# Layer 1's attention: column factors on GpSimd, tables two steps later, ready sums between the values' halves, last results in the values' banks

## The chip, the cores and the metric

The kernel runs on one core of one Trainium2 chip. The metric is the device time of one execution in microseconds (us), the lower the better; the time of a kernel is the median of its timed runs. One further execution is recorded by the hardware profiler, and every view of the profile and of the trace is of that execution. The engines are TensorE (PE for its matmuls, PEld for its weight loads), VectorE (DVE), ScalarE (ACT), GpSimd (POOL) and the queue SP, which only issues DMAs. The engines run beside each other; each works through its own instructions in order and waits on semaphores for what other engines make.

## The reference

Two layers on 4096 nodes with 512 features, all in float32. Layer 0 is an attention over edges with full scores; layer 1, which the change touches, has 8 heads of 64 columns. Cut to what matters:

```python
h = relu(layernorm(x)); x = x + L0(h, adj)
h = relu(layernorm(x)); x = x + L1(h, adj)

def L1(data, connectivity, W, b, src_proj, trg_proj):
    data1 = (data @ W.T + b).reshape(N, H, D)          # N, H, D = 4096, 8, 64
    src = einsum('nhd,xhd->nh', data1, src_proj)
    trg = einsum('nhd,xhd->nh', data1, trg_proj)
    e = src.T[:, :, None] + trg.T[:, None, :]
    e = where(e >= 0, e, 0.01 * e) + connectivity[None]
    scores = softmax(e, axis=-1)
    return einsum('hnm,hmd->hnd', scores, data1.transpose(1, 0, 2))
```

The connectivity that layer 1 is given is adj itself, added to the scores.

## The kernel before, in words

Layer 0 comes first (lines 89 to 687): layernorm and the two products, the scores of all pairs, and a second pass that weighs them; at its end (`tail`, `values`, `logits`) layer 1's values are left in the tile `sup` (4096 rows of 8 heads of 64 columns, also called `va`), and the two logits of each node in `s_n` and `t_m`.

Layer 1's attention (from line 692) never forms the exponent of a sum. For row n and column m of one head, exp of the leaky sum is a product of a factor of the row, a factor of the column, and max(z[n], g[m]), where z is made from the row's logit and `g_m`, `d_m` from the column's. So one score is `max(z, g) * d * exp(adj)`.

The work is cut into **8 groups**: 4 blocks of 1024 rows (`WL`) by 2 sets of 4 heads (`HG`). Each group goes through 32 **steps**, one for each 128 columns m, so there are 256 steps. In one step:

- SP loads the 128x1024 tile `e` of adj (`load`, L789), three steps ahead.
- ACT makes `ex = exp(e)` into PSUM (`exps`, L807; one buffer of two banks), `e3`, the same with head 3's factor of the column in it (`last_exps`, L817), and `rl`, relu(d z - d g) for head 0 (`relus`, L835). In four steps of a group (`BY_LOG`) head 0's weights come from one exp of a sum that a DMA has formed instead (L824, L825, L832).
- VectorE makes the four weight tiles `pr3, pr0, pr1, pr2` of 128x1024 (`weigh`, L838 to L852), each by one scalar_tensor_tensor: max(z, g) times ex or e3 (L849), and for head 0 (rl - ngd) times ex (L846). Heads 0 and 3 come out with their factor d of the column in them; heads 1 and 2 do not.
- For heads 1 and 2 the factor d goes into the values instead, in place: `scale` (L803) multiplies the 128x64 block of `va` by d. That is done once for each set of heads, so in groups 0 and 1 only, two steps ahead.
- GpSimd adds up pr3 over the columns (`acc3`, L856 and L858), and for 19 of the 32 steps (`BY_DMA`) it issues a DMA that adds pr0 to one of two sums in SBUF (`acc00` and `acc01`, L863 and L865). The last step's pr3 is left out of the sum.
- TensorE (`gather`, L867) multiplies the four weight tiles with the values: 32 instructions into four PSUM banks `pv00` to `pv11` (L881), first the pair of heads (3, 0), then the pair (1, 2). A matmul uses 32 columns of the array, so four run beside each other, and a matmul in float32 is two instructions. Then come the **denominators** into the bank `dn` (L886): heads 1 and 2 each step with the weights d, head 0 in the 13 steps that are not `BY_DMA`. In a group's last step come also pr3 of that step, and the sums acc01, acc00 and acc3. `side` changes which half of the array a step begins with, so that what one step leaves of one half can run beside the next step's start in the other.

After a group ACT copies the four banks (`os`, L910) and dn (`od`, L916). TensorE turns `od` (L920) and, one block of 128 rows a step, `os` (L936); ACT divides (L960), and a DMA of GpSimd adds to the layer's input. After the last group `finish_last` does the same at once: eight results of 128x256, `pts[0..7]`; the even ones VectorE multiplies and adds (L998), the odd ones ACT multiplies (L995), and VectorE adds the layer's input to them (L1003, L1004); four DMAs of SP write the output. `pts[0..3]` lie in the four banks of the values, `pts[4..7]` in one tile of two banks that held `ex`.

What sets the order around the change: the block runs under a manual schedule, so the order of the code is written out by hand. The start is lines 1013 to 1051: the rows' factors z of heads 3, 1, 2, 0 (`row_factors`, VectorE at L1028 and ACT at L1029), the columns' factors (L1032 to L1041), rl of step 0 (`relus(0, 0)`, L1042), memsets and copies on GpSimd (L1044 to L1047), the products of step 0 in the order of heads 3, 1, 2, 0, and the factors of steps 0 and 1. Then the loop (L1053 to L1064) issues for each step s: `load` of step s+3, `logs` of s+5, `exps` and `weigh` of s+1, `factors` and `scale` of s+2, `gather` of s, and one piece of `ending`: in group 0 that is `tables` (L750: the tables of z and u for all later groups, made from `s_n` on ACT and TensorE and written to DRAM by GpSimd's DMAs), afterwards `finish` of the group before.

Of the kernel before, what the change touches and what calls it, by code (L numbers as in the profile page):

```python
# [8 lines left out]
FP = mybir.dt.float32  # L9
# [6 lines left out]
P = 128  # L16
# [12 lines left out]
def kernel(  # L29
# [334 lines left out]
    with tc.tile_pool(name="c_a", bufs=11) as adjp, tc.tile_pool(name="c_b", bufs=4) as ebp, tc.tile_pool(  # L364
# [231 lines left out]
        def values(t):  # L596
            v = sup[:, t, :]
            nc.vector.tensor_tensor(v, vps.pop(t), wt["b"], ALU.add)
            for key, name in (("t", "ex"), ("s", "mk")):
                prs[t, key] = wkp.tile([P, BL], FP, name=name)  # L600
                eng = nc.vector if t == NT - 1 and key == "t" else nc.gpsimd
                eng.tensor_tensor(prs[t, key], v, wt[key], ALU.mult)
# [118 lines left out]

    HV = WL // BL
    JT = BL // P
    Q = P // 4
# [3 lines left out]
    with tc.tile_pool(name="p", bufs=2) as prp, tc.tile_pool(name="rl", bufs=2) as rlp, tc.tile_pool(  # L731
# [66 lines left out]
        def scale(i, m):  # L798


            if i < H // HG:
                for h in range(groups[i][1] * HG + 1, groups[i][1] * HG + 3):
                    nc.scalar.activation(va[:, m, h, :], va[:, m, h, :], AF.Copy, scale=d_m[:, h, m:m + 1])  # L803

        def exps(i, m):
            x_ = p_x.tile([P, WL], FP, name="ex")
# [31 lines left out]
        def weigh(i, m, order=ORDER):  # L838
            h = groups[i][1] * HG
            x_ = ex.pop((i, m))  # L840
            for k in order:
                if (i, m, k) in pr:
                    continue
                w = prp.tile([P, WL], FP, name=f"pr{k}", bufs=3 if k == 0 else 2)
                if k == 0:
                    nc.vector.scalar_tensor_tensor(w, rl.pop((i, m)), ngd_m[:, h // HG, m:m + 1], x_,  # L846
                                                   op0=ALU.subtract, op1=ALU.mult)
                else:
                    nc.vector.scalar_tensor_tensor(w, zs_[i, k], g_m[:, h + k, m:m + 1],  # L849
                                                   e3.pop((i, m)) if k == 3 else x_,  # L850
                                                   op0=ALU.max, op1=ALU.mult)
                pr[i, m, k] = w  # L852
            w = pr[i, m, 3]
            if m == 1:
                acc[i, 3] = acp.tile([P, WL], FP, name="acc3", bufs=1)
                nc.gpsimd.tensor_tensor(acc[i, 3], pr[i, 0, 3], w, ALU.add)  # L856
            elif 1 < m < NT - 1:
                nc.gpsimd.tensor_tensor(acc[i, 3], acc[i, 3], w, ALU.add)  # L858
            if m in BY_DMA:
                n = BY_DMA.index(m)  # L860
                if n < 2:
                    acc[i, 0, n] = acp.tile([P, WL], FP, name=f"acc0{n}", bufs=1)
                    nc.gpsimd.dma_start(acc[i, 0, n], pr[i, m, 0])  # L863
                else:
                    nc.gpsimd.dma_start(acc[i, 0, n % 2], pr[i, m, 0], accum_op=ALU.add)  # L865

        def gather(i, m):  # L867
            b, g = groups[i]
            last = m == NT - 1
            if m == 0:  # L870
                pv[i] = ([[p_v.tile([P, BL], FP, name=f"pv{c}{q}") for q in range(HV)] for c in range(2)],
                         p_v.tile([P, BL], FP, name="dn"))
            v, dn = pv[i]
            by_pe = [u for u in range(NT) if u not in BY_DMA]
            side = sum(u < m for u in by_pe) % 2
            for c, pair in enumerate(((3, 0), (1, 2))):
                for q in range(HV):
                    for r in (side, 1 - side):
                        k = pair[r]
                        for c0 in range(0, D, Q):  # L880
                            nc.tensor.matmul(v[c][q][r * D + c0:r * D + c0 + Q, :],  # L881
                                             va[:, m, g * HG + k, c0:c0 + Q],
                                             pr[i, m, k][:, q * BL:(q + 1) * BL], start=(m == 0), stop=last)

            def den(r, w, src, q, **fl):
                nc.tensor.matmul(dn[r * Q:r * Q + w.shape[1], :], w, src[:, q * BL:(q + 1) * BL], **fl)  # L886

            for r in (side, 1 - side):
                for q in range(HV):
                    hk = g * 2 + r  # L890
                    den(r * HV + q, d0_m[:, hk, m, :] if m else d0_0[:, hk, :], pr[i, m, r + 1], q,
                        start=(m == 0), stop=False)
            if m in by_pe:
                for q in range(HV):
                    den(side * HV + q, zo[:, 1 - side:3], pr[i, m, 0], q, start=False, stop=False)
            if last:
                for q in range(HV):
                    den(HV + q, zo[:, 1:3], pr[i, m, 3], q, start=False, stop=False)
                for q in range(HV):
                    den(q, zo[:, 1:3], acc[i, 0, 1], q, start=False, stop=False)  # L900
                for r, a in enumerate((acc[i, 0, 0], acc[i, 3])):
                    for q in range(HV):
                        den(r * HV + q, zo[:, 1:3], a, q, start=False, stop=True)
            for k in range(HG):
                pr.pop((i, m - 1, k), None)
            if last:
                os_ = [[osp.tile([P, BL], FP, name=f"os{c}{q}") for q in range(HV)] for c in range(2)]
                for c in range(2):
                    for q in range(HV):
                        nc.scalar.copy(os_[c][q], v[c][q])  # L910
                late[i] = os_, dn
# [60 lines left out]
        def finish_last(i):  # L972

            ys = [ep.tile([P, WT // 2, HG, D], FP, name="e") for _ in range(2)]
            for n in range(2):
                nc.sync.dma_start(ys[n], part(x1, i, n * WT // 2, WT // 2))
            yield
            dens = denominators(i)
            os_ = next(dens)
            pts = [p_v.tile([P, HG, D], FP, name=f"pv{c}{q}") for q in range(HV) for c in range(2)]  # L980
            xs = p_x.tile([P, 4, HG, D], FP, name="ex")
            pts += [xs[:, n, :, :] for n in range(4)]
            for t in range(4):
                turn(os_, t, pts[t])
            next(dens)
            for t in range(4, WT):
                turn(os_, t, pts[t])
            rd = next(dens)
            o = [prp.tile([P, WT // 2, HG, D], FP, name=f"pr{n + 1}") for n in range(2)]
            for t in range(WT):  # L990
                n, j = divmod(t, WT // 2)
                to, y = o[n][:, j, :, :], ys[n][:, j, :, :]
                if t % 2:
                    for r, k in enumerate(ORDER):
                        nc.scalar.activation(to[:, k, :], pts[t][:, r, :], AF.Copy, scale=share(rd, t, r))  # L995
                else:
                    for r, k in enumerate(ORDER):
                        nc.vector.scalar_tensor_tensor(to[:, k, :], pts[t][:, r, :], share(rd, t, r), y[:, k, :],  # L998
                                                       op0=ALU.mult, op1=ALU.add)
                if t % 2 == 0 and t:  # L1000
                    n, j = divmod(t - 1, WT // 2)
                    to, y = o[n][:, j, :, :], ys[n][:, j, :, :]
                    nc.vector.tensor_tensor(to, to, y, ALU.add)  # L1003
            nc.vector.tensor_tensor(o[1][:, WT // 2 - 1, :, :], o[1][:, WT // 2 - 1, :, :],  # L1004
                                    ys[1][:, WT // 2 - 1, :, :], ALU.add)
            for t in range(0, WT, 2):
                n, j = divmod(t, WT // 2)
                nc.sync.dma_start(part(out, i, t, 2), o[n][:, j:j + 2, :, :])
            yield
# [29 lines left out]
        for k in (1, 2, 0):  # L1039
            row_factors(k)  # L1040
        nc.vector.scalar_tensor_tensor(ngd_m, g_m[:, 0::HG, :], -1.0, d_m[:, 0::HG, :], op0=ALU.mult, op1=ALU.mult)  # L1041
        relus(0, 0)  # L1042
        for t, val in ((d0_0, 0.0), (d0_m, 0.0), (zo[:, 0:2], 0.0), (zo[:, 2:3], 1.0)):
            nc.gpsimd.memset(t, val)  # L1044
        for g in range(H // HG):
# [8 lines left out]
        for s in range(len(steps)):  # L1054
            for f, ahead in stages:
                if s + ahead < len(steps):
                    f(*steps[s + ahead])
            if s == 0:
                ending = tables()
            elif s % NT == 0:  # L1060
                ending = finish(s // NT - 1)
            if s == len(steps) - 2:
                ending = finish_last(len(groups) - 1)
            next(ending, None)  # L1064
# [36 lines left out]
```

## Time and profile before

| what | value |
|---|---|
| median of 3 runs | 2959.15 us (2958.06 to 2962.82) |
| the profiled execution's own time | 2957.07 us |
| its span | 2955.3 us |
| TensorE, busy share of the span | 99% (2911.4 us) |
| VectorE | 86% (2534.6 us) |
| ACT | 45% (1325.5 us) |
| GpSimd | 47% (1380.0 us) |
| layer 1's attention, first product of VectorE to the end | 1727.9 to 2955.3 us |
| first long run of value matmuls (L881) | from 1733.21 us |
| last denominator (L886) ends | 2943.39 us |
| L881, matmuls of the values | 8192 instructions, 594 ns each |
| L886, denominators with d of heads 1 and 2, or of pr0 | 1984 instructions of the commonest form, 592 ns each |
| L803, column factors on ACT | 128 instructions, 333 ns each |
| L858, additions on GpSimd | 232 instructions, 2406 ns each |

How to read it: the span is what lies between the first and the last instruction that the profiler saw; the time is about 1.8 us longer. Busy shares are means over all stages. Layer 1's attention is the last 1227 us of the span, and its busy times by stretch are a view of their own. In a row of the trace "pr<-z,g_m,e" names the tile written and the tiles read, "128x1024 f32" the shape, "x2" that two equal instructions are merged, and a bracket gives the idle time of the engine before it and what ended that. Matmuls are pipelined: a mean of 594 ns is a latency, and four column groups work at a time.

### The profile page before, as it was taken

How to read it: one execution, taken by the hardware profiler on the slowest of the kernel's cores; microseconds unless marked ns; L12 is line 12 of the kernel's file. 1: busy time of each engine (PE TensorE's matmuls, PEld its weight loads, DVE VectorE, ACT ScalarE, POOL GpSimd, SP SyncE). 2: the span in 40 equal slices, each digit the busy share in tenths (PEclk: the TensorE clock that was granted, in tenths of full speed). 3: DMA queues.
4: the chain of work that ended last, by engine and by line, in shares of the span. 5: the costliest groups of instructions: out<-in, count | busy, mean ns of one | idle time of the engine just before them, and what ended most of it. 6: DMA issues, size and time to landing. Idle time of an engine off the chain costs nothing.

```text
span 2955.3 us, 42955 instructions
## 1 busy us (share of the span) xinstructions
PE 2911.4 (99%) x15179; PEld 1137.7 (38%) x15179; DVE 2534.6 (86%) x3584; ACT 1325.5 (45%) x1822; POOL 1380.0 (47%) x1043
## 2 busy tenths in 40 slices
PE   8999999999999999999999989999999999999998
PEld 4444444444444444444444423323222322232222
DVE  5435777778888998998996789999999999999998
ACT  2211111111121221221221068888777777777776
POOL 3401111113444444444444756565757575757574
PEclk9999999999999999999999999999999999999999
DMA  5525666667876766756653259696969696979795
GB/s 181 172 78 200 223 218 225 226 218 187 205 178 162 177 161 187 186 166 180 190 167 127 61 152 242 187 258 188 256 191 249 194 250 204 243 202 243 208 232 153
DMA packets 485160, 570.89 MB, mean 193 GB/s; under 512 B 265080, under 2 KB 315288, under 8 KB 484944
## 3 DMA queue, kind: packets, MB, share of 16 engines
q1 hardware_dynamic: 431920, 406.70, 45.8%
q0 software_dynamic: 51008, 157.51, 23.2%
q10 hardware_dynamic: 2016, 3.93, 0.4%
q8 instruction: 119, 1.95, 0.3%
q14 instruction: 97, 0.79, 0.1%
HBM read 415.76 MB, written 72.55 MB: 165 GB/s over the span
## 4 chain that ended last, share of the span: by engine, by line
PE 92%; DVE 4%; ACT 2%; DMA 1%; issue 1%; SPq 0%; POOL 0%; DVEq 0%; ACTq 0%; POOLq 0%
PE po L480 29%; PE pv L881 27%; PE pe L331 15%; PE dn L886 9%; PE po L591 4%; PE ps L196 3%; PE pe L203 3%; DVE pr L849 2%; PE pt L936 1%; ACT e L817 1%; DMA acc<-pr 1%; DMA xt<-in_x_dram 0%; DVE acc_z L154 0%; DVE pt L441 0%; PE pt L920 0%
## 5 line engine op out<-in xcount | busy, mean ns | idle before, releaser
L881 PE MATMUL pv<-pr,sup 128*32 128x512 f32 x8192 | 1010.0, 594 | 9.0 <-POOL d_m L1046 5.4
L480 PE MATMUL po<-sup,at 128*128 128x512 f32 x2048 | 887.2, 594 | 3.8 <-DVE at L450 3.8
L858 POOL TENSOR_TENSOR acc<-acc,pr 128x1024 f32<-128x1024 f32 x232 | 558.2, 2406 | 318.1 <-DVE pr L849 317.8
L849 DVE SCALAR_TENSOR_TENSOR pr<-z,g_m,ex 128x1024 f32<-128x1024 f32 x512 | 631.0, 1273 | 5.2 <-ACT ex L807 4.1
L480 PEld LDWEIGHTS po<-sup,at 128*128 128x128 f32 x2048 | 387.1, 190 | 483.2 <-issue 446.3
L460 POOL TENSOR_TENSOR racc<-racc,ex 128x512 f32<-128x512 f32 x240 | 362.3, 1510 | 385.3 <-ACT ex L444 383.8
L881 PEld LDWEIGHTS pv<-pr,sup 128*32 128x32 f32 x8192 | 286.7, 110 | 593.2 <-issue 533.6
L444 ACT ACTIVATE ex<-d 128x512 f32<-128x512 f32 x256 | 160.5, 630 | 624.7 <-DVE d L442 616.5
L331 PE MATMUL pe<-he_t,he_t 128*128 128x512 f32 x896 | 386.4, 592 | 0.0
L807 ACT ACTIVATE ex<-e 128x1024 f32<-128x1024 f32 x256 | 263.0, 1027 | 227.2 <-DVE pr L849 226.6
L849 DVE SCALAR_TENSOR_TENSOR pr<-z,g_m,e 128x1024 f32<-128x1024 f32 x256 | 328.9, 1285 | 9.9 <-PE pv L881 5.9
L886 PE MATMUL dn<-pr,d_m 128*2 128x512 f32 x1984 | 335.6, 592 | 0.0
L817 ACT ACTIVATE e<-e,ld_m 128x1024 f32<-128x1024 f32 x256 | 291.0, 1137 | 6.5 <-DMA e<-in_adj_t_dram 6.3
L846 DVE SCALAR_TENSOR_TENSOR pr<-rl,ngd_m,ex 128x1024 f32<-128x1024 f32 x224 | 285.0, 1273 | 1.6 <-ACT ex L807 1.2
L835 ACT ACTIVATE rl<-z,ngd_m,d_m 128x1024 f32<-128x1024 f32 x224 | 275.0, 1228 | 0.0
L450 DVE TENSOR_TENSOR at<-ex,a 128x512 f32<-128x512 f32 x256 | 189.5, 740 | 71.1 <-ACT ex L444 48.0
L331 PEld LDWEIGHTS pe<-he_t,he_t 128*128 128x128 f32 x896 | 169.2, 190 | 210.1 <-issue 190.5
L335 POOL DMA_DIRECT2D e_d<-es x144 | 78.4, 545 | 364.8 <-ACT es L334 359.2
L334 ACT COPY es<-pe 128x512 f32<-128x512 f32 (+2 forms) x144 | 79.1, 550 | 377.2 <-PE pe L331 377.2
L442 DVE TENSOR_TENSOR d<-pt,mk 128x512 f32<-128x512 f32 x256 | 177.0, 691 | 8.8
L336 DVE CUSTOM_DVE_ANT_0 mk<-pe,mk 128x512 f32<-128x512 f32 (+2 forms) x144 | 93.0, 645 | 98.9 <-ACT es L334 98.8
L435 DVE TENSOR_SCALAR mk<-a 128x512 f32<-128x512 f32 x256 | 128.5, 502 | 2.2 <-DMA a<-in_adj_t_dram 2.2
(186 smaller groups left out, 2564.9 us busy)
## 6 DMA issues: line engine op xcount, KB each, us to landing
e<-in_adj_t_dram SPq DMA_DIRECT2D x256, 512.0 KB, 5.5
acc<-pr POOLq DMA_DIRECT2D x152, 512.0 KB, 5.7
a<-in_adj_t_dram SPq DMA_DIRECT2D x256, 256.0 KB, 3.8
ar<-in_adj_dram SPq DMA_DIRECT2D x120, 256.0 KB, 3.0
e_d<-es POOLq DMA_DIRECT2D x120, 256.0 KB, 3.1
eb<-e_d SPq DMA_DIRECT2D x456, 64.0 KB, 3.0
ac<-in_adj_t_dram SPq DMA_DIRECT2D x112, 256.0 KB, 3.5
et<-e_d SPq DMA_DIRECT2D x112, 256.0 KB, 3.8
```

Source lines behind the costliest of these rows:

```text
L331: nc.tensor.matmul(pe[:, :w], he_t[i][:, k, (t % TB) * P:(t % TB + 1) * P], he_t[j][:, k, BL - w:], start=(k == 0), stop=(k == KC - 1))
L450: nc.vector.tensor_tensor(w, e, aj.pop((b, m)), ALU.mult)
L460: nc.gpsimd.tensor_tensor(racc, racc, e, ALU.add)
L480: nc.tensor.matmul(po[j], w[:, j * P:(j + 1) * P], sup[:, m, :], start=(m == 0), stop=last)
L807: nc.scalar.activation(x_, ra.pop((i, m)), AF.Exp)
L817: nc.scalar.activation(x_, ra[i, m], AF.Exp, bias=ld_m[:, h // HG, m:m + 1])
L835: nc.scalar.activation(r, zs_[i, 0], AF.Relu, bias=ngd_m[:, h // HG, m:m + 1], scale=d_m[:, h, m:m + 1])
L846: nc.vector.scalar_tensor_tensor(w, rl.pop((i, m)), ngd_m[:, h // HG, m:m + 1], x_, op0=ALU.subtract, op1=ALU.mult)
L849: nc.vector.scalar_tensor_tensor(w, zs_[i, k], g_m[:, h + k, m:m + 1], e3.pop((i, m)) if k == 3 else x_, op0=ALU.max, op1=ALU.mult)
L858: nc.gpsimd.tensor_tensor(acc[i, 3], acc[i, 3], w, ALU.add)
L881: nc.tensor.matmul(v[c][q][r * D + c0:r * D + c0 + Q, :], va[:, m, g * HG + k, c0:c0 + Q], pr[i, m, k][:, q * BL:(q + 1) * BL], start=(m = ...
L886: nc.tensor.matmul(dn[r * Q:r * Q + w.shape[1], :], w, src[:, q * BL:(q + 1) * BL], **fl)
```

## The change

In groups 0 and 1 the column factors of the values (`scale`) are multiplied in by GpSimd's tensor_scalar instead of ACT's activation. For step 0, rl is made by one VectorE tensor_scalar, max(z, g) times d, ahead of the four products, instead of ACT's relu, and head 0's product of that step becomes a plain tensor_tensor. `tables` starts at step 2 instead of step 0. GpSimd now adds the last step's pr3 into acc3 too; in a group's last step TensorE takes the sums acc00 and acc3, and pr0 of that step, between the two pairs of heads, and after the second pair the denominators of heads 1 and 2 and the sum acc01; the separate denominators of pr3 are gone. In `finish_last` the eight results lie in four tiles of one bank each in the values' banks: results 0 and 2, 1 and 3, 4 and 6, 5 and 7 share a tile.

```diff
@@ scale @@
-                    nc.scalar.activation(va[:, m, h, :], va[:, m, h, :], AF.Copy, scale=d_m[:, h, m:m + 1])
+                    nc.gpsimd.tensor_scalar(va[:, m, h, :], va[:, m, h, :], d_m[:, h, m:m + 1], None, ALU.mult)
@@ weigh @@
-                if k == 0:
+                if k == 0 and (i, m) == (0, 0):
+                    nc.vector.tensor_tensor(w, rl.pop((i, m)), x_, ALU.mult)
+                elif k == 0:
                     nc.vector.scalar_tensor_tensor(w, rl.pop((i, m)), ngd_m[:, h // HG, m:m + 1], x_,
                                                    op0=ALU.subtract, op1=ALU.mult)
...
-            elif 1 < m < NT - 1:
+            elif m > 1:
                 nc.gpsimd.tensor_tensor(acc[i, 3], acc[i, 3], w, ALU.add)
@@ gather @@
-            for c, pair in enumerate(((3, 0), (1, 2))):
+
+            def values(c):
                 for q in range(HV):
                     for r in (side, 1 - side):
-                        k = pair[r]
+                        k = ((3, 0), (1, 2))[c][r]
...
+            values(0)
+            if last:
+                for r, a in enumerate((acc[i, 0, 0], acc[i, 3])):
+                    for q in range(HV):
+                        den(r * HV + q, zo[:, 1:3], a, q, start=False, stop=False)
+                if m in by_pe:
+                    for q in range(HV):
+                        den(side * HV + q, zo[:, 1 - side:3], pr[i, m, 0], q, start=False, stop=False)
+            values(1)
             for r in (side, 1 - side):
                 for q in range(HV):
                     hk = g * 2 + r
                     den(r * HV + q, d0_m[:, hk, m, :] if m else d0_0[:, hk, :], pr[i, m, r + 1], q,
-                        start=(m == 0), stop=False)
-            if m in by_pe:
+                        start=(m == 0), stop=(last and r == 1))
+            if m in by_pe and not last:
                 for q in range(HV):
                     den(side * HV + q, zo[:, 1 - side:3], pr[i, m, 0], q, start=False, stop=False)
             if last:
                 for q in range(HV):
-                    den(HV + q, zo[:, 1:3], pr[i, m, 3], q, start=False, stop=False)
-                for q in range(HV):
-                    den(q, zo[:, 1:3], acc[i, 0, 1], q, start=False, stop=False)
-                for r, a in enumerate((acc[i, 0, 0], acc[i, 3])):
-                    for q in range(HV):
-                        den(r * HV + q, zo[:, 1:3], a, q, start=False, stop=True)
+                    den(q, zo[:, 1:3], acc[i, 0, 1], q, start=False, stop=True)
@@ finish_last @@
-            pts = [p_v.tile([P, HG, D], FP, name=f"pv{c}{q}") for q in range(HV) for c in range(2)]
-            xs = p_x.tile([P, 4, HG, D], FP, name="ex")
-            pts += [xs[:, n, :, :] for n in range(4)]
+            pts = []
+            for n in range(2):
+                two = [p_v.tile([P, 2, HG, D], FP, name=f"pv{n}{c}") for c in range(2)]
+                pts += [two[c][:, j, :, :] for j in range(2) for c in range(2)]
@@ the start @@
         nc.vector.scalar_tensor_tensor(ngd_m, g_m[:, 0::HG, :], -1.0, d_m[:, 0::HG, :], op0=ALU.mult, op1=ALU.mult)
-        relus(0, 0)
+        rl[0, 0] = rlp.tile([P, WL], FP, name="rl")
+        nc.vector.tensor_scalar(rl[0, 0], zs_[0, 0], g_m[:, 0, 0:1], d_m[:, 0, 0:1], ALU.max, ALU.mult)
@@ the loop @@
             if s == 0:
+                ending = iter(())
+            elif s == 2:
                 ending = tables()
             elif s % NT == 0:
                 ending = finish(s // NT - 1)
```

## The prediction

> **What bounds the kernel now.** I read four views, in this order. First the table of stretches of layer 1's attention: length, then busy time of PE, PEld, DVE, ACT and POOL with instruction counts, the granted TensorE clock, the DMA share and GB/s.
>
> ```profile
> 1733.20:1771.00 37.80, 37.79 (x316) 10.21 (x320) 36.37 (x31) 32.94 (x54) 23.56 (x16) 0.94 0.63 170
> 1771.00:1811.00 40.00, 39.45 (x364) 11.60 (x356) 40.00 (x34) 32.53 (x45) 26.70 (x17) 1.00 0.86 212
> 1811.00:1850.00 39.00, 38.18 (x355) 12.96 (x356) 38.60 (x34) 33.84 (x46) 27.77 (x18) 1.00 1.03 278
> 1850.00:1884.60 34.60, 34.60 (x324) 11.96 (x320) 34.08 (x30) 29.23 (x43) 14.24 (x7) 1.00 0.61 177
> 1884.60:1922.00 37.40, 37.12 (x330) 11.19 (x326) 37.36 (x33) 33.46 (x60) 25.44 (x16) 1.00 0.69 185
> 2035.70:2186.70 151.00, 151.00 (x1376) 44.27 (x1372) 148.91 (x126) 116.64 (x138) 95.06 (x57) 1.00 0.84 224
> ```
>
> The first four rows are group 0 of eight, the fifth the start of group 1, the last all of group 2. TensorE is busy without a gap in group 2, and VectorE is only 2.1 us short of it. So TensorE sets the end from group 1 on, VectorE is a close second, ACT and GpSimd have room. In group 0 TensorE is idle 0.55 + 0.82 = 1.37 us, and 0.28 us at the start of group 1. So an edit that only frees ACT can win about 1.65 us, and anything more must shorten the first step, the tail or TensorE's own work.
>
> Second, the timeline of the first step, VectorE and ACT (start, length, instruction):
>
> ```profile
> 1727.90 1.28 DVE L849 SCALAR_TENSOR_TENSOR pr<-z,g_m,e 128x1024 f32<-128x1024 f32 x1
> 1729.10 2.47 DVE L849 SCALAR_TENSOR_TENSOR pr<-z,g_m,ex 128x1024 f32<-128x1024 f32 x2
> 1731.88 1.28 DVE L846 SCALAR_TENSOR_TENSOR pr<-rl,ngd_m,ex 128x1024 f32<-128x1024 f32 x1 [0.31 <-ACT rl L835]
> 1733.39 1.28 DVE L849 SCALAR_TENSOR_TENSOR pr<-z,g_m,e 128x1024 f32<-128x1024 f32 x1 [0.24 <-ACT e L817]
> 1735.91 1.28 DVE L846 SCALAR_TENSOR_TENSOR pr<-rl,ngd_m,ex 128x1024 f32<-128x1024 f32 x1 [1.24 <-ACT ex L807]
> ```
> ```profile
> 1729.53 1.04 ACT L1029 ACTIVATE z<-u 128x1024 f32<-128x1024 f32 x1
> 1730.60 1.24 ACT L835 ACTIVATE rl<-z,ngd_m,d_m 128x1024 f32<-128x1024 f32 x1
> ```
>
> The three products of heads 3, 1, 2 run while ACT still makes z of head 0; only head 0's product (L846) waits for rl. Products follow each other every 1.19 us, so a full step of four takes VectorE 4.77 us. VectorE then loses 0.24 and 1.24 us behind a loaded ACT.
>
> Third, the tail, VectorE's last results:
>
> ```profile
> 2945.64 1.63 DVE L998 SCALAR_TENSOR_TENSOR pr<-pv,rd,e 128x64 f32<-128x64 f32 x8
> 2947.18 0.42 DVE L1003 TENSOR_TENSOR pr<-pr,e 128x256 f32<-128x256 f32 x1
> 2947.51 0.85 DVE L998 SCALAR_TENSOR_TENSOR pr<-ex,rd,e 128x64 f32<-128x64 f32 x4
> 2949.42 0.86 DVE L998 SCALAR_TENSOR_TENSOR pr<-ex,rd,e 128x64 f32<-128x64 f32 x4 [0.72 <-ACT pr L995]
> 2951.27 0.43 DVE L1004 TENSOR_TENSOR pr<-pr,e 128x256 f32<-128x256 f32 x1 [0.66 <-ACT pr L995]
> ```
>
> Out of the shared tile "ex" VectorE and ACT take turns; out of "pv" both run at once. Fourth, the groups of GpSimd, for the prices below.
>
> **The change, part by part.** All sums go against the profiled execution: span 2955.3 us, time 2957.07 us. The three timed runs have a median of 2959.15 us, 2.08 above it; I carry the difference over to that median.
>
> *(a) rl of step 0 on VectorE.* The new instruction stands ahead of weigh(0, 0) in the code, and inside this block every engine ran in code order in the trace. It reads z of head 0, which ACT finishes at 1730.57. Queued behind it on VectorE are the three products that now run from 1727.90. So: start 1730.62; tensor_scalar of 128x1024 as at L1028, 0.751 us, next start 0.67 later at 1731.29; heads 3, 1, 2 at 1731.29, 1732.48, 1733.68; head 0's plain product at 1734.87 (a tensor_tensor of half the size takes 0.691 us at L442, so I keep 1.2), end 1736.1. Now that end is 1733.16. TensorE's second head of step 0 starts **2.95 us later**. ACT's next ex waits for the one PSUM tile and comes at 1736.15 to 1737.15, head 0 of step 1 at 1737.25 in place of 1735.91: VectorE itself is only 1.34 us later from there, because its 0.24 and 1.24 us stalls go. TensorE is thus 1.6 us further behind VectorE than now, which fills its 1.37 us of idle time in group 0. Net at the end of group 0: 2.95 - 1.37 = **+1.6**. ACT loses 1.23 us of work there, which nobody waits for any more.
>
> *(b) Column factors on GpSimd.* 128 activations of 0.333 us leave ACT, 128 tensor_scalars of 128x64 come to GpSimd, two a step in groups 0 and 1. The trace has none of that form. Low end: a copy of 128x4, 0.190 us (L1047). High end: the copy of 128x64 at L1046, 0.774 us, strided and run beside VectorE's first product. Between them a copy of 128x512 took 0.622 us (L247); on the line from the first, (0.622 - 0.190) / 508 per element, 64 elements take 0.24. I take 0.25, nearest to that row. GpSimd's step is then 2.41 (L858) + 0.87 (L865) + 0.5 = 3.8 of 4.77 us; 3.7 at the low end, 4.8 at the high, where it is full. Queued behind the factors are the next addition and the issue of the next accumulating DMA; these only free buffers. TensorE needs the factors two steps after they are issued. ACT's relief lets the copy of the denominators (od) come earlier, which removes the 0.28 at the start of group 1: **-0.3**.
>
> What GpSimd may cost is VectorE's time. The addition starts 1.43 us after head 3's product and ends at 3.8, the DMA issue at 4.65, so in 19 of 32 steps the two factors meet the next head-3 product at 4.77, which reads z and e3, both in SBUF. What such a meeting costs:
>
> ```profile
> 2924.34 2.39 POOL L858 TENSOR_TENSOR acc<-acc,pr 128x1024 f32<-128x1024 f32 x1 [2.66 <-DVE pr L849]
> 2926.22 1.59 DVE L849 SCALAR_TENSOR_TENSOR pr<-z,g_m,e 128x1024 f32<-128x1024 f32 x1
> ```
>
> 0.51 us of overlap made the product 0.31 us longer; at 1833.01 an overlap of 0.27 cost 0.08. Two groups of 19 steps at 0 to 0.31 are 0 to 11.8 us of VectorE; its slack of 2.1 us a group hides the first 4.2 (about 0.11 a step). I take 0.1 a step and **+0.5** for what shows; the ends are 0 and +7.6. The Trainium skill, "SBUF — State Buffer", section "Who interferes with whom", speaks against this edit: a VectorE instruction with two SBUF inputs and a GpSimd instruction that reads SBUF exclude each other for the whole instruction, the later one blocked. By that rule a product would wait at most one factor (0.25), or a factor a whole product; the sum would be about +5 if the product always lost, and -0.2 if it always won.
>
> *(c) tables from step 2.* Eight activations (0.307 each), their transposes, copies, one exp and three GpSimd DMA issues (0.88, 0.87, 0.87) move two steps, about 9 us, later, into the same kind of gaps. Their results are first loaded at step 20. Nothing passes a load on SP. **0** (bounds -0.3 to +0.3, one transpose pair on TensorE).
>
> *(d) Ready sums between the halves.* GpSimd adds the last step's head 3 (2.41 us, eight times) in a gap of 12 to 13 us in front of L856; TensorE drops two of 14 denominator products a group, four instructions. In group 2's last step the product was made at 1.28 us from 2175.72 and TensorE began that step at 2180.40, so the sum is ready 1.0 us before TensorE starts; if that lead went, the second half would wait for VectorE anyway. But does TensorE gain? Four instructions on four column groups take 0.43 us; these take turns by halves of the array. Before, the last step and what is left of step 30 make 16 half blocks that alternate, 8 x 0.86 = 6.9 us, as the chain shows (3.43 + 3.42). Now there are 15, but the last one (acc01) uses the same half as the next group's first values, so half the array stands idle: 8 x 0.86 again. **0**; lower end 7 x 0.43 = -3.0 if it packs. Two waits go: VectorE's 0.5 us per group on head 3's buffer, off the path.
>
> *(e) Last results in the values' banks.* VectorE and ACT now read separate tiles. From 2945.64 VectorE needs 16 products at 0.193 and four additions of about 0.36: 4.55, to 2950.2 in place of 2951.7. ACT's 16 at 0.217 end at 2949.1, ahead. The 3.6 us from the last addition to the end stay. **-1.5** (bounds -2.1, ACT and VectorE perfectly apart, to 0).
>
> Sum: +1.6 - 0.3 + 0.5 + 0 + 0 - 1.5 = **+0.3**: 2957.4 for the profiled execution, 2959.4 against the median.
>
> **Rivals.** *Order:* if the factor of (a) is placed behind the three products, head 0 ends at 1733.46 (+0.3), VectorE gains 1.3, and TensorE's idle 1.37 goes: -1.0 in place of +1.6, 2956.9. For it: pick (L778) ran ahead of an earlier line at the boundary of two blocks; against: inside the block no instruction did. *Packing:* (d) pays its 3.0: 2956.4. Against it: half blocks fit the measured 6.85 us. Both together: 2953.9. *Slower, the shared read:* the head-3 products lose 0.3 a step to the factors: (11.8 - 4.2) = +7.6 in place of +0.5, 2966.5; it decides from 0.11 us a step. For it the 1.59 row; against it, the typical overlap is nearer 0.25, where the rows show 0.05 to 0.08.
>
> **How the numbers follow.** Forecast 0.55, order 0.14, packing 0.13, both 0.06, shared read 0.12. About 0.2% (5.9 us) is what a measurement of this kernel can tell from no change. "Both" lies at that bound and I count it as faster, the shared read as slower, the rest within: 0.06, 0.82, 0.12. The range takes in the case "both" with scatter below and most of the shared read: 2953 to 2966.
>
> **What would show it.** (a) right: VectorE's first product after 1731, TensorE's first long run of pv near 1736; wrong: a product at 1727.9. (b): GpSimd tensor_scalar near 0.25 us, head-3 products of groups 0 and 1 with a mean under 1.38 us; (d): groups 2 to 6 still 151.05 us apart; 150.6 means packing. (e): no wait of VectorE on ACT after 2946, and about 10.4 us from the last dn to the end in place of 11.9. A GpSimd price near 0.8, or a TensorE wait on GpSimd in front of pv, would make the whole wrong.

## The result, and the profile after

The changed kernel takes **2964.18 us** (median of 19 runs, 2962.2 to 2968.54) beside 2958.06 us (19 runs, 2954.96 to 2962.82) for the kernel before on the same chip. The ratio is 1.0023, 95% interval 1.0016 to 1.0029: about 6 to 7 us slower, 4.7 to 8.6 by the interval. The forecast was 2959.4, so the time lies 4.8 us above it, inside the range, at the edge of "within 0.2%" and nearest to the rival of the shared read (2966.5). As a difference from the kernel before, the forecast was +0.3 and the measurement +6.1: with 19 runs the median of before is 1.1 us lower than the one that the forecast was added to. The profiled execution took 2964.42 us, span 2962.6.

The stretches of layer 1's attention in the changed kernel, columns as in the prediction (length, then busy PE, PEld, DVE, ACT, POOL). The first three rows have the limits of three rows shown of before; the last is all of group 2, which starts 8 us later here:

```profile
1771.00:1811.00 40.00, 40.00 (x373) 11.62 (x369) 40.00 (x35) 28.61 (x30) 39.95 (x34) 1.00 0.93 210
1811.00:1850.00 39.00, 37.45 (x340) 11.91 (x336) 39.00 (x32) 27.71 (x26) 39.00 (x33) 1.00 1.02 263
1850.00:1884.60 34.60, 33.78 (x312) 11.14 (x307) 34.54 (x28) 24.58 (x24) 31.97 (x29) 1.00 0.69 193
2044.10:2195.10 151.00, 151.00 (x1372) 47.46 (x1368) 148.69 (x126) 116.71 (x138) 97.32 (x58) 1.00 0.84 224
```

GpSimd, the fifth busy time, went from 26.70 and 27.77 to 39.95 and 39.00 us: it is full. VectorE, nearly full before (40.00 and 38.60), is full too, and TensorE is idle for 1.55 and 0.82 us in the second and third rows, where it was idle for 0.82 and 0. Group 2, which has no factors, is as before but for GpSimd's one addition more (97.32 in place of 95.06 us).

Three groups of instructions from 1725 to 2035 us, which is nearly all of groups 0 and 1 (busy us, mean ns, idle before), and below them two rows of the kernel before from the same stretch:

```profile
L859 POOL TENSOR_TENSOR acc<-acc,pr 128x1024 f32<-128x1024 f32 x59 | 162.2, 2750 | 8.6 <-DVE pr L850 8.5
...
L802 POOL TENSOR_SCALAR sup<-sup,d_m 128x64 f32<-128x64 f32 x128 | 125.0, 1410 | 0.2
L850 DVE SCALAR_TENSOR_TENSOR pr<-z,g_m,e 128x1024 f32<-128x1024 f32 x64 | 93.1, 1455 | 0.0
```
```profile
L858 POOL TENSOR_TENSOR acc<-acc,pr 128x1024 f32<-128x1024 f32 x58 | 139.7, 2409 | 79.6 <-DVE pr L849 79.3
...
L849 DVE SCALAR_TENSOR_TENSOR pr<-z,g_m,e 128x1024 f32<-128x1024 f32 x66 | 84.7, 1284 | 2.0 <-ACT os L910 1.1 <-PE pv L881 0.7 <-ACT e L817 0.2
```

A column factor takes 1410 ns in the mean, not 250; the addition 2750 in place of 2410; the head-3 product 1455 in place of 1284. GpSimd's idle time before its additions falls from 79.6 to 8.6 us. The positions at which TensorE turns the denominators (L920, now L926) place the loss: the way from the first row factor (L1028, L1035) to the end of group 0 is 5 us longer, group 1 takes 154.97 us in place of 151.05, groups 2 to 7 together are 0.2 us longer than before, and the tail is 1.1 us shorter.

How a loss arises, from the timeline of GpSimd and VectorE in group 0 (start, length, row), with VectorE's row at the spot of the first product in the kernel before below:

```profile
1833.12 1.31 POOL L824 DMA_DIRECT2D lg<-in_adj_t_dram  x1
...
1833.74 3.12 POOL L859 TENSOR_TENSOR acc<-acc,pr 128x1024 f32<-128x1024 f32 x1
1835.17 2.79 DVE L850 SCALAR_TENSOR_TENSOR pr<-z,g_m,e 128x1024 f32<-128x1024 f32 x1
...
1840.42 1.44 POOL L866 DMA_DIRECT2D acc<-pr  x1
1841.08 2.35 POOL L802 TENSOR_SCALAR sup<-sup,d_m 128x64 f32<-128x64 f32 x2
1841.45 1.27 DVE L850 SCALAR_TENSOR_TENSOR pr<-z,g_m,e 128x1024 f32<-128x1024 f32 x1
...
1843.00 2.77 POOL L859 TENSOR_TENSOR acc<-acc,pr 128x1024 f32<-128x1024 f32 x1
```
```profile
1833.01 1.36 DVE L849 SCALAR_TENSOR_TENSOR pr<-z,g_m,e 128x1024 f32<-128x1024 f32 x1
```

Read the last four rows of the changed kernel first, a normal step: two factors meet the head-3 product, the product keeps its 1.27 us, and the pair, 0.86 us when free, takes 2.35. The addition behind it starts later. GpSimd's rows overlap: the pair's row begins 0.37 us ahead of the product, while the issue of the accumulating DMA before it (L866) still runs to 1841.86. So the start of a GpSimd row does not tell when its work begins, and part of the means above is queueing behind the row before. The first rows are a step of `BY_LOG`: VectorE makes three products in place of four, GpSimd has a load to issue, and the late addition is still running when the next head-3 product is due. Now the product waits, 2.79 us in place of 1.36 at this spot before. The meeting costs VectorE nothing where the factor loses and 1.5 us where the addition wins. The Trainium skill, "SBUF — State Buffer", section "Who interferes with whom", states that whichever of the two comes later is blocked for the whole instruction. The first rows agree: the addition ends at 1836.86, and the product that began during it ends 1.1 us behind that. In the last rows the starts do not tell which came first.

The long products have a place. In each of groups 0 and 1 the products of steps 18, 22 and 26, right behind the `BY_LOG` steps 17, 21 and 25, take 2.64 to 2.79 us: 8.9 us of the 11.1 by which products are longer than before in these two groups. Behind step 29, after the last accumulating DMA of a group, the product takes 1.33 and 1.32. The other 2.2 us lie on six products of 1.44 to 1.93 us, one in group 0 and five in group 1. Shortly before each of them GpSimd has one more DMA to issue, for a `BY_LOG` load (L824) or a result of group 0 (L969).

The start and the tail stand in two more pieces of VectorE's timeline in the changed kernel:

```profile
1729.93 0.81 DVE L1050 TENSOR_SCALAR rl<-z,g_m,d_m 128x1024 f32<-128x1024 f32 x1 [2.61 <-ACT z L1036]
1730.66 1.28 DVE L850 SCALAR_TENSOR_TENSOR pr<-z,g_m,e 128x1024 f32<-128x1024 f32 x1
...
1734.24 1.21 DVE L845 TENSOR_TENSOR pr<-rl,ex 128x1024 f32<-128x1024 f32 x1
```
```profile
2954.16 1.63 DVE L1005 SCALAR_TENSOR_TENSOR pr<-pv,rd,e 128x64 f32<-128x64 f32 x8
2955.70 0.42 DVE L1010 TENSOR_TENSOR pr<-pr,e 128x256 f32<-128x256 f32 x1
2956.03 0.85 DVE L1005 SCALAR_TENSOR_TENSOR pr<-pv,rd,e 128x64 f32<-128x64 f32 x4
```

The products of heads 3, 1, 2 wait 2.61 us for z of head 0, as worked out; the tail has no wait on ACT left.

### The profile page after: what moved, and what is told of

Read it like the earlier page. It is cut to its first block, busy times and chain, and to the rows that moved or that the text cites. A ratio compares the mean times of both kernels' runs of the same rounds, so it can differ in the third digit from the quotient of the medians.

```text
span 2962.6 us, 42943 instructions
## 1 busy us (share of the span) xinstructions
PE 2914.6 (98%) x15147; PEld 1146.7 (39%) x15147; DVE 2545.9 (86%) x3585; ACT 1295.6 (44%) x1693; POOL 1494.5 (50%) x1179
## 4 chain that ended last, share of the span: by engine, by line
PE 82%; POOL 6%; DVE 5%; DMA 3%; issue 2%; ACT 1%; SPq 1%; DVEq 0%; POOLq 0%; ACTq 0%
PE po L480 29%; PE pv L883 20%; PE pe L331 15%; PE dn L888 7%; PE po L591 4%; PE ps L196 3%; POOL acc L859 3%; DVE pr L850 3%; PE pe L203 3%; DMA acc<-pr 2%; POOL sup L802 1%; POOL acc L866 1%; PE pt L942 1%; DVE pr L847 0%; SPq L409 0%
## 5 line engine op out<-in xcount | busy, mean ns | idle before, releaser
L883 PE MATMUL pv<-pr,sup 128*32 128x512 f32 x8192 | 1024.2, 595 | 15.2 <-DVE pr L850 12.0
L859 POOL TENSOR_TENSOR acc<-acc,pr 128x1024 f32<-128x1024 f32 x240 | 597.7, 2490 | 264.9 <-DVE pr L850 263.1
L883 PEld LDWEIGHTS pv<-pr,sup 128*32 128x32 f32 x8192 | 293.5, 110 | 598.2 <-issue 521.0
L850 DVE SCALAR_TENSOR_TENSOR pr<-z,g_m,e 128x1024 f32<-128x1024 f32 x256 | 339.6, 1327 | 4.2 <-PE pv L883 4.0
L866 POOL DMA_DIRECT2D acc<-pr x136 | 133.1, 978 | 2.2 <-DVE pr L850 1.2
```

Of the source, the lines that this page charges most:

```text
L883: nc.tensor.matmul(v[c][q][r * D + c0:r * D + c0 + Q, :], va[:, m, g * HG + k, c0:c0 + Q], pr[i, m, k][:, q * BL:(q + 1) * BL], start=(m = ...
```

## The experiments

Every kernel was timed beside the kernel before on one chip, whose medians were 2957.71 (first four), 2957.62 (next four) and 2958.53 us (last four). "Over before" is the difference of the medians, with the ratio's 95% interval. "Long products" is the time by which head-3 products of groups 0 and 1 over 1.41 us exceed 1.28 us, added up in the profiled execution; it is 0 in the kernel before.

| kernel | us | over before | ratio | long products, groups 0 + 1 |
|---|---|---|---|---|
| changed kernel | 2964.18 | +6.1 | 1.0016 to 1.0029 | 4.7 + 6.4 |
| e1 factors on ACT | 2958.65 | +0.9 | 0.9992 to 1.0010 | 0 |
| e2 start undone | 2960.89 | +3.2 | 1.0003 to 1.0021 | 4.8 + 6.2 |
| e3 factors ahead of the DMA | 2964.95 | +7.2 | 1.0013 to 1.0036 | 0.5 + 0.3 |
| e4 factors alone | 2964.41 | +6.7 | 1.0013 to 1.0031 | 4.9 + 5.3 |
| e5 tail alone | 2956.77 | -0.9 | 0.9987 to 1.0006 | 0 |
| e6 late factors on ACT | 2958.83 | +1.2 | 0.9996 to 1.0013 | 0.3 + 1.7 |
| e7 early factors on ACT | 2963.95 | +6.3 | 1.0013 to 1.0031 | 4.5 + 4.5 |
| e8 rl behind, factors on ACT | 2955.43 | -2.2 | 0.9986 to 1.0003 | 0 |
| e9 sums and tables alone | 2957.44 | -1.1 | 0.9987 to 1.0005 | 0 |
| e10 start alone | 2959.99 | +1.5 | 0.9992 to 1.0009 | 0 |
| e11 two factors in one | 2958.85 | +0.3 | 0.9993 to 1.0011 | 0.7 + 0.7 |
| e12 rl behind, and the tail | 2955.62 | -2.9 | 0.9984 to 1.0001 | 0 |

**Which part loses.** e1, e2 and e4 take one part away or put one in; e3 keeps the work and changes its order on GpSimd.

e1:
```diff
-                    nc.gpsimd.tensor_scalar(va[:, m, h, :], va[:, m, h, :], d_m[:, h, m:m + 1], None, ALU.mult)
+                    nc.scalar.activation(va[:, m, h, :], va[:, m, h, :], AF.Copy, scale=d_m[:, h, m:m + 1])
```

> The changed kernel with the 128 column factors back on ACT; all else as changed. Theory A (shared read): a factor and a head-3 product, which both read SBUF, shut each other out; GpSimd gets full in groups 0 and 1, its late additions then hold up head-3 products. Of the 5.0 us that group 0 got longer A gives 3.4 to this and of group 1 all 3.9: expected 2957 (7.3 under the changed kernel), long head-3 products gone from groups 0 and 1, GpSimd back to about 27 of 40 us. Theory B (start): the loss comes from rl of step 0 on VectorE, which VectorE never makes good: expected 2963 to 2964, group 1 still near 155. Theory C (only the sheer amount of GpSimd work counts) gives the same as A here.

Measured 2958.65: 5.2 us back by the differences from before, and no long product left. That is 1.7 us above what A gave, which e1's interval still holds. The profiled execution (2960.16, the slowest of the eleven) also shows 4.7 us of ACT waits for loads of adj in group 0, so its positions are not compared. B falls.

e2:
```diff
-        rl[0, 0] = rlp.tile([P, WL], FP, name="rl")
-        nc.vector.tensor_scalar(rl[0, 0], zs_[0, 0], g_m[:, 0, 0:1], d_m[:, 0, 0:1], ALU.max, ALU.mult)
+        relus(0, 0)
...
-                if k == 0 and (i, m) == (0, 0):
-                    nc.vector.tensor_tensor(w, rl.pop((i, m)), x_, ALU.mult)
-                elif k == 0:
+                if k == 0:
```

> The changed kernel with only the start undone: rl of step 0 on ACT again and head 0's product as before. Theory A: the start costs 1.6 to 3.0, so 2961.2 to 2962.6; group 1 stays near 155 us. If GpSimd sets the pace of group 0, the earlier start is partly lost again and the gain is under 1.6. Theory B: 5 us or more come back, 2959 or less, and group 1 is 151 again.

Measured 2960.89, 2.9 under the changed kernel by the differences from before. Group 1 stays at 154.8 us. Both speak for A.

e4 is the diff of e1 the other way round, on the kernel before.

> The kernel before with the column factors on GpSimd and nothing else changed. Theory A: 5 to 7 us over before, 2963 to 2966, factors with a mean over 1 us and long head-3 products in groups 0 and 1. Theory B: within 1 us of before.

Measured 2964.41, +6.7, factors with a mean of 1418 ns: the factors alone make the whole loss. In e4's trace groups 0 and 1 are 2.9 and 4.0 us longer than before. On the scale of the first row factor its head-3 products fall behind those of the kernel before by 1.4 to 1.5 us at steps 19, 23 and 27 of group 0 and 19 and 27 of group 1, each right behind a long product, and far less elsewhere.

e3:
```diff
             elif m > 1:
                 nc.gpsimd.tensor_tensor(acc[i, 3], acc[i, 3], w, ALU.add)
+            if (i, m) > (0, 0) and (i, m) != steps[-1]:
+                scale(*steps[steps.index((i, m)) + 1])
             if m in BY_DMA:
...
-        stages = ((load, 3), (logs, 5), (exps, 1), (weigh, 1), (factors, 2), (scale, 2), (gather, 0))
+        stages = ((load, 3), (logs, 5), (exps, 1), (weigh, 1), (factors, 2), (gather, 0))
```

> The changed kernel with the two factors of a step issued between GpSimd's addition and its accumulating DMA, so that they come some 3.8 us after the head-3 product in place of 4.7, ahead of the next head-3 product. The same instructions on the same engines. Theory A: the mean factor falls from 1.41 to about 0.45 to 0.6 us, GpSimd is free 5 us or more in 40, and 5 to 7 of the 7.3 us come back: 2957 to 2959. Theory C (amount of work): the same time as the changed kernel, 2964. Theory B: 2964.

Measured 2964.95, from only six runs that spread from 2958.93 to 2968.32: in the median none of the time came back, against A as first put. The groups of instructions show why that isn't simply theory C:

```profile
L850 DVE SCALAR_TENSOR_TENSOR pr<-z,g_m,e 128x1024 f32<-128x1024 f32 x64 | 83.0, 1297 | 0.8 <-PE pv L885 0.7
...
L802 POOL TENSOR_SCALAR sup<-sup,d_m 128x64 f32<-128x64 f32 x128 | 72.5, 693 | 0.0
```

The mean factor halves to 693 ns, and head-3 products are nearly as short as before. In the profiled execution group 1 takes 152.21 us, 2.8 less than in the changed kernel, so there most of its loss is gone; group 0 is 1.1 us longer than there. In it another wait took the place. Of ACT's waits in group 0 the longest:

```profile
ACT pr L831 <- DMA acc<-pr: 4.4, 1, 4.4
```

The accumulating DMA, now behind the factors, releases one of the three buffers of pr0. In step 25, where ACT writes pr0 itself, it waits 4.43 us for that; the exp behind it is late, and VectorE idles 3.66 us. That wait was 0.6 us in the changed kernel and 0 before. So there seem to be two ways in which a late GpSimd costs time; the second rests on this one wait. The DMA that it waits for is that of step 22: its issue took 2.38 us in place of 0.87 before, and it landed 9.0 us after that, its counterparts 7.3 (before) and 7.1 us (changed kernel). So late issue and slow transfer both have a part; the exact shares stay open.

**Where it loses.** A full step of 4.77 us leaves 3.5 us outside the head-3 product; the addition and two free factors take 2.39 + 0.86 = 3.25. A `BY_LOG` step has one product less, 3.6 us, and leaves 2.3. The four such steps are 17, 21, 25 and 29; that is theory A2. (In the traces the products behind the first three are the long ones, as said above.) e6 puts the factors from step 16 on back on ACT, e7 those up to step 15:

```diff
+                    if m < 16:
                         nc.gpsimd.tensor_scalar(va[:, m, h, :], va[:, m, h, :], d_m[:, h, m:m + 1], None, ALU.mult)
+                    else:
+                        nc.scalar.activation(va[:, m, h, :], va[:, m, h, :], AF.Copy, scale=d_m[:, h, m:m + 1])
```

> The changed kernel with the factors of steps 16 to 31 of groups 0 and 1 on ACT, those of steps 0 to 15 on GpSimd. Theory A2: a full step of four products leaves GpSimd 3.5 us of 4.8 outside VectorE's head-3 product, which holds an addition of 2.4 and two factors of 0.43; the shorter steps 17, 21, 25 and 29, with three products and a load issued by GpSimd, do not, and all of the loss falls there. Expected: 4.5 to 6 us under the changed kernel, 2958 to 2959.5 on the scale of a kernel before at 2957.7. Theory A as first put (each of the 64 steps loses alike): half comes back, about 3 us, 2961. Theory C (amount of GpSimd work): the same as A, half.

> The mirror image: factors of steps 0 to 15 on ACT, those of steps 16 to 31 on GpSimd. Theory A2: nearly all of the loss stays, 0 to 1.5 us under the changed kernel, 2962.5 to 2964. Theories A as first put and C: half comes back, 2961.

Measured 2958.83 and 2963.95. The same number of GpSimd instructions costs nothing that can be told from e1 in the first half of a group, and everything in the second. The groups from 1811 to 1890 us, the second half of group 0, in e6 and then in e7:

```profile
L862 POOL TENSOR_TENSOR acc<-acc,pr 128x1024 f32<-128x1024 f32 x16 | 38.7, 2420 | 21.4 <-DVE pr L853 21.4
L853 DVE SCALAR_TENSOR_TENSOR pr<-z,g_m,e 128x1024 f32<-128x1024 f32 x18 | 23.2, 1287 | 0.0
```
```profile
L862 POOL TENSOR_TENSOR acc<-acc,pr 128x1024 f32<-128x1024 f32 x15 | 41.5, 2768 | 2.6 <-DVE pr L853 2.6
...
L853 DVE SCALAR_TENSOR_TENSOR pr<-z,g_m,e 128x1024 f32<-128x1024 f32 x17 | 26.3, 1548 | 0.0
```

The addition's idle time of 21.4 us shrinks to 2.6, and the head-3 product gets 0.26 us longer in the mean. In the first half of e6's group 0 GpSimd is nearly as full as in the changed kernel (its addition idles for 3.7 us in 76, 2.6 there), and only one product of 1.59 us pays for it; in group 1 four pay 1.7 us together. Theory C, which gave both half of the loss, falls with that, and A as first put too. The halves differ in more than the short steps, so it is the place of the long products, steps 18, 22 and 26 in e7 too, that ties the loss to them.

**The price of a factor.** e11 makes the two factors of a step in one instruction:

```diff
-                for h in range(groups[i][1] * HG + 1, groups[i][1] * HG + 3):
-                    nc.gpsimd.tensor_scalar(va[:, m, h, :], va[:, m, h, :], d_m[:, h, m:m + 1], None, ALU.mult)
+                h = groups[i][1] * HG + 1
+                nc.gpsimd.tensor_tensor(va[:, m, h:h + 2, :], va[:, m, h:h + 2, :],
+                                        d_m[:, h:h + 2, m:m + 1].to_broadcast([P, 2, D]), ALU.mult)
```

> The changed kernel with the two factors of a step in one GpSimd instruction of 128x128 (a product of two tensors, the second spread along the columns) in place of two of 128x64. Estimate from the addition of 128x1024 at 2.39 and the small copies at 0.19: about 0.5 us for both in place of 0.86. Theory A2 (GpSimd's need in the shorter steps sets the loss): 0.36 us less in each of the 32 late steps, a fourth to a half of the 5.3 us comes back: 2961.5 to 2963. If the loss hangs on the meeting of any factor with the head-3 product, however short: 2964.

Measured 2958.85, 5.8 us better than the changed kernel by the differences from before, more than either theory gave. Its timeline around a `BY_LOG` step:

```profile
1812.43 0.72 POOL L802 TENSOR_TENSOR sup<-sup,d_m 128x128 f32<-128x128 f32 x1
1812.78 1.22 POOL L825 DMA_DIRECT2D lg<-in_adj_t_dram  x1
1812.84 1.40 DVE L851 SCALAR_TENSOR_TENSOR pr<-z,g_m,e 128x1024 f32<-128x1024 f32 x1
1814.16 2.46 DVE L851 SCALAR_TENSOR_TENSOR pr<-z,g_m,ex 128x1024 f32<-128x1024 f32 x2
1814.40 2.39 POOL L860 TENSOR_TENSOR acc<-acc,pr 128x1024 f32<-128x1024 f32 x1 [0.39 <-DVE pr L851]
```

The one instruction has started before the product, so the product waits for what is left of it and is 0.12 us longer, and GpSimd is free again when the addition may start. With two instructions the second mostly came after the product had begun and waited for all of it (the median factor of the changed kernel takes 1764 ns). The first one's row is mostly as long, though it begins 0.2 to 0.4 us ahead of the product; why it loses there is not shown. Free of a product the one takes 0.39 us against 2 x 0.43: of the 1.6 us between 2.35 and 0.72 only 0.5 are the price; the rest is the meeting with the product.

**The other parts.** e5 is the diff of `finish_last` alone, e9 those of `gather`, of the last addition and of `tables`, e10 that of the start, each on the kernel before.

> The kernel before with the last results in the values' banks and nothing else changed. Expected from the changed kernel's trace, where the way from the last group's denominators to the end is 1.2 us shorter than before: 1.2 under before (0.9 to 1.5), in the profile no wait of VectorE on ACT between its last results. Rival: VectorE's time between the last results was hidden by the stores, 0.

> The kernel before with the ready sums between the values' halves and the tables from step 2 on, nothing else changed. Both stand at 0 in the sum on record: within 0.15% of before (2953.5 to 2962), groups 2 to 6 as far apart as before. Packing rival: 3.0 less. Tables rival: the table's bytes and loads come two steps later, into the stretch in which the DMA engines are full, and cost 1 to 2 us in groups 0 and 1.

> The kernel before with only the start changed: rl of step 0 on VectorE ahead of the three products. The sum on record has +1.6. With e1_factors_act at +0.94 over before, which holds the shorter tail (-0.9 to -1.2), the start is worth +1.8 to +2.2 by that run: 2959.5 to 2960 where before is 2957.7. If the start is harmless by itself, 2957.7.

Measured -0.9, -1.1 and +1.5 us, none of them told from 0 by its interval. They lie at or near what the expectations have, e9 nearer 0 than the packing's -3.0, which its interval still holds. The traces say more: in e9 groups 2, 4 and 6 take 151.05 us as before and 3 and 5 are no shorter, against the packing; its group 0 is 0.1 us longer, and group 1 1.2, which is no sign of the tables, since e10, where they are not moved, has the same 1.2. In e10 group 0 is 1.4 us longer. With e4's +6.7 the four medians add up to +6.2, the changed kernel has +6.1; that this fits so closely is luck, since each of the four is uncertain by more than 2 us either way.

e8 (e1's diff, with rl made behind the three products) and e12 (the same start and the new tail on the kernel before):
```diff
                 if k == 0 and (i, m) == (0, 0):
+                    r = rlp.tile([P, WL], FP, name="rl")
+                    nc.vector.tensor_scalar(r, zs_[0, 0], g_m[:, 0, 0:1], d_m[:, 0, 0:1], ALU.max, ALU.mult)
-                    nc.vector.tensor_tensor(w, rl.pop((i, m)), x_, ALU.mult)
+                    nc.vector.tensor_tensor(w, r, x_, ALU.mult)
```

> The changed kernel with the factors on ACT (as in e1_factors_act) and step 0's factor rl on VectorE behind the three products of heads 3, 1, 2 in place of ahead of them. By the sum on record that order is worth -2.6 against the order ahead (+1.6 to -1.0): 2956 on the scale of a kernel before at 2957.7, and 1.5 to 2.5 under before. If the start's later clock or the loads of the table set the pace of group 0 whatever VectorE does, it is level with e1_factors_act, 2958.6.

> The kernel before with two edits: step 0's rl on VectorE behind the three products, and the last results in the values' banks; no factors on GpSimd, no ready sums, no moved tables. By e8_rl_behind (-2.2) and the sum on record (-1.0 and -1.2): 2955.5 where before is 2957.7. If sums and tables carry part of e8's gain: 2956.5.

Measured 2955.43 and 2955.62, both as expected. VectorE's start in e8, whose layer 0 ended 4 us later in this execution:

```profile
1731.98 1.28 DVE L852 SCALAR_TENSOR_TENSOR pr<-z,g_m,e 128x1024 f32<-128x1024 f32 x1
...
1735.56 0.81 DVE L846 TENSOR_SCALAR rl<-z,g_m,d_m 128x1024 f32<-128x1024 f32 x1
1736.41 1.22 DVE L847 TENSOR_TENSOR pr<-rl,ex 128x1024 f32<-128x1024 f32 x1
1737.54 1.28 DVE L852 SCALAR_TENSOR_TENSOR pr<-z,g_m,e 128x1024 f32<-128x1024 f32 x1
```

No product waits for rl or ex here. TensorE's long run starts 9.37 us after the first row factor (8.98 before, 11.95 in the changed kernel), and group 0 ends 1.0 us earlier than before on that scale (1.4 in e12); group 1 takes 0.9 us longer again (1.6 in e12). From the first row factor to the end the profiled executions of e8 and e12 are 0.6 and 0.8 us shorter than before, that of e5 with the tail alone 1.5. So the traces show the gain of the order in group 0, but none in the whole. Both kernels are 2 to 3 us under before in their medians, with intervals that end at 1.0003 and 1.0001: probably faster, not shown to be, and 8 to 9 us better than the changed kernel.

## Why the prediction was right or wrong

- **(a) Start: right in mechanism and size.** TensorE's long run came 2.97 us later on the scale of the first row factor (2.95 forecast), head 0 of step 1 1.32 later (1.34). e10 has +1.5 for it, +1.4 at the end of group 0 in its trace, the sum +1.6; the interval of the time (-0.08% to +0.09%) holds 0 as well. The order rival was wrong for the change as made. Its place behind the products gains what it said up to the end of group 0 (-1.0 in e8); that this lasts to the end of the kernel is not shown.
- **(b) Factors: wrong, and this is the whole miss.** Two steps failed. The price: "I take 0.25, nearest to that row" measured 0.43 when free. That alone would have left room, 2.41 + 0.87 + 0.86 = 4.14 of 4.77 us, but only in a full step: the sum never asked about the `BY_LOG` step of 3.6 us, behind which most of the long products lie. The step that decided was "these only free buffers", said of the addition and the DMA issue behind the factors. An addition that starts late holds up the next head-3 product, 1.5 us at a time, and a late DMA held up ACT through pr0 once, in e3. "+0.5" measured +6.7 (e4). The rival of the shared read had the size, +7.6, by another road: it let every one of 38 products lose 0.3 us, while in the trace most products lost nothing (1.27 us), the factors lost in most steps, and six products behind short steps paid 8.9 of 11.1 us.
- **The range held by luck.** It takes in the time only because its upper end was drawn to hold most of the shared read, a case given 0.12; the central sum had the factors at +0.5 in place of +6.7.
- The bounds were also read from the wrong row. The "high end" of 0.774 us was the mean of two copies of 0.30 and 1.25 us, the second beside VectorE's first product; in the changed kernel, where no product runs beside them, they take 0.29 and 0.24. So it was a blocked instruction and no price, and it held the warning that a small GpSimd instruction loses that meeting.
- **od earlier, -0.3:** the copy of the denominators no longer holds TensorE between groups 0 and 1, but TensorE had become late by more than that.
- **(c), (d): right.** Groups 2, 4 and 6 still take 151.05 us, 3 and 5 up to 0.6 more in either kernel, and e9 has -1.1 us, not told from 0; the packing rival is refuted by the distances.
- **(e) Tail: right in mechanism, a little smaller:** 1.1 us less from the last denominator to the end (11.86 to 10.72; 10.4 forecast), and -0.9 in e5. VectorE's part took 4.50 us (4.55 forecast); what missed is "the 3.6 us from the last addition to the end stay": they became 4.0, in e5 too.
- The signs set out beforehand for (a), (d) and (e) came; for (b) both failed: 1.41 us in place of "near 0.25", and 1455 ns in place of a mean "under 1.38 us".

## What to carry to other kernels

Before work goes to GpSimd, count its free time in the shortest step, without the stretches in which VectorE reads two SBUF tiles, and ask of every instruction behind the new one which product it can meet when it is late. A busy share over a whole stretch (27 of 40 us here) hides both. Where small pieces must go there, one instruction can be worth more than two with the same work: here 5.8 us.

## What was not expected of the hardware

- Free of VectorE, GpSimd's product of two tensors of 128x128 took 0.39 us, its tensor_scalar of 128x64, half the elements and one tensor, 0.43 us, and its copy of 128x64 0.24 to 0.30 us. The Trainium skill, "GPSIMD Engine Reference", section "4.1 Engine selection", has GpSimd about twice as slow as VectorE on operations with two inputs and at about line rate on those with one. The addition of 128x1024 agrees (2.39 us, VectorE's product of two tensors of that size, one of them in PSUM, 1.21); the small operation with one input does not: 0.43 us beside 0.20 for VectorE's tensor_scalar of 128x64 (L1040), and here the measurement decides.
- One meeting can cost either side: two factors 0.86 us free and 2.35 against a head-3 product; the product 1.28 us free and 2.79 against an addition.
